# Linear attention with the routing of its tokens: the same steps in six slots instead of thirteen

## Chip, cores and metric

One core of one Trainium2 chip runs the whole kernel. The metric is the time of one execution on the device in microseconds; three runs before the change took 4580.45, 4585.04 and 4587.49, so the median is 4585.04.

## What is computed

The reference is a chain of sixteen residual blocks on 4096 tokens of 128 features (16 sequences of 256). Two neighbours matter here, a linear attention and the mixture of experts behind it:

```python
# linear attention (x is already normalised)
q = elu(x @ Wq.T) + 1;  k = elu(x @ Wk.T) + 1;  v = x @ Wv.T      # 16 heads of 8
kv = einsum('bhnd,bhne->bhde', k, v);  k_state = k.sum(axis=2)
attn = einsum('bhnd,bhde->bhne', q, kv) / max(q . k_state, 1e-6)
local = conv of width 3 over the sequence
return (attn + local) @ Wp.T + bp

# mixture of experts (x is already normalised)
logits = einsum('nc,ec->ne', xt, gate_w)                          # 8 experts
top_vals, top_idx = top_k(logits, 2);  top_w = softmax(top_vals)
expert e: (silu(xt @ w1[e].T) * (xt @ w2[e].T)) @ w3[e].T
out = sum over the two chosen experts of weight * expert(xt)
```

## The kernel before, in words

Activations stay on the chip, features on the partitions, in eight chunks of 512 tokens (two sequences each). `self.x` holds the residual stream, `self.ha` the normalised copy. A stage of the kernel is a list of steps, each a function of a chunk. `slots` (L1819) writes the order out by hand: in slot k, step i works on chunk k - i. The scheduler is told to keep this order (`manual_schedule`), and each engine then takes its instructions in the order in which they were written.

The linear attention (`linear`, L1947) has eight steps: three of the layer norm (`norm`: mean by a matmul, square, matmul, logarithm and exponential, multiply; for chunks 0 to 4 the stage before has done them, and they are empty), `project` (three projections, elu, the convolution), `sums` (k and v to `kv`), `heads` (q and `kv`, and the division), `join` (a transpose back, added to the convolution) and `out` (output projection, added to `x`).

Behind them come, as `last`, the eight steps that route the tokens to the experts. They are made by `Sending.steps` (L3545), and called "lead" steps, since they belong to the next block but are written into this stage:

- `norm(0)` to `norm(2)`, called `centre`, `spread` and `scale` below: the norm of the new `x`. Here the square is made on ScalarE.
- `compare` (L3566): the logits (TensorE), copied out on VectorE; `ahead`, which expert's logit is above which (VectorE, L3574), multiplied by a triangle on GpSimd (L3578); the maximum subtracted and `Exp` on ScalarE.
- `choose` (L3585): ranks from two sums over `ahead`, marks of the first and second expert, the two weights; all on VectorE down to the reciprocal (L3605), then two small instructions on GpSimd (L3606, L3607) that fill the weight and the token number into the row `out`.
- `place` (L3613): small matmuls count how many tokens went to each expert before this one; from that VectorE makes the row number `idx` (L3633).
- `turn` (L3636): four transposes of the normalised tokens, copied by ScalarE into `out`.
- `scatter` (L3645): eight indirect DMAs from GpSimd's queue (L3649), which write the 2 x 512 rows into the DRAM buffer `rows`, sorted by expert.

After the stage `table` (L3655) makes a small table, from which expert and row each tile of the experts starts, and `experts` (L2126) loads rows (L2145) and expert weights (L2147) through the queue of SyncE. Its first load waits for all rows to be stored.

So before, a chunk that enters at `project` in slot k is in `scatter` in slot k + 12: thirteen slots. Slot 2 is the first that has work (`project` of chunk 0), slot 22 the last (`scatter` of chunk 7). Within a slot, `slots` first writes the eight attention steps, the last one first, and then the eight lead steps, the last one first: `scatter`(c), `turn`(c+1), `place`(c+2), `choose`(c+3), `compare`(c+4), and so on. The number in brackets is the chunk.

Tiles rotate through small sets of buffers: two of most, three of `idx`, four of `out`; eight banks of the matmuls' result memory ("ps") are shared by all steps. A step that takes a buffer waits until its earlier reader is done.

Of the kernel before, what the change touches and what calls it, by code (L numbers as in the profile page):

```python
# [21 lines left out]
NCH = NT // CH  # L22
# [1627 lines left out]
class Fast(Net):  # L1650
# [168 lines left out]
    def slots(self, n, *steps, last=()):  # L1819
# [3 lines left out]
        with self.tc.manual_schedule():  # L1823
            self.logs()
            for k in range(n + len(both) - 1):
                for i in (*reversed(range(len(steps))), *reversed(range(len(steps), len(both)))):
                    if 0 <= k - i < n and k < n + len(both) - 1:
                        both[i](k - i)

    def lead(self, pool, bank="ps", tables=False):
# [114 lines left out]
    def linear(self, w):  # L1947
        x, h0 = self.x, self.ha
        nc = self.nc
        with ExitStack() as st:  # L1950
            p = self.stage(st, "n2", 2)
            qs, ks, kvs, os, ls = {}, {}, {}, {}, {}
            norm = [lambda c, i=i: self.norm_x_step(p, c, i) for i in range(3)]

            def elu1(ps, tag, bufs):
                e = p.tile([P, CH], F32, tag=tag, name=tag, bufs=bufs)
                self.act(e, ps, AF.Relu, scale=-1.0)
                self.act(e, e, AF.Exp, scale=-1.0)
                self.stt(e, ps, 0.0, e, ALU.max, ALU.add)
                return e  # L1960

            def project(c):
                s = self.chunk(c)
                pq, pk, pv = self.bank(), self.bank(), self.bank()
                self.mm(pq, w["Wq"], h0[:, s])
                for t in range(4):
                    ht = h0[:, c * CH + t * P : c * CH + t * P + P]
                    self.mm(pk[:, t * P : t * P + P], ht, w["Wk"])
                    self.mm(pv[:, t * P : t * P + P], ht, w["Wv"])
                qs[c] = elu1(pq, "q", 3)  # L1970
                k = elu1(pk, "k", 2)
                v = p.tile([P, 4, P + 1], F32, tag="v", name="v")
                self.act(v[:, :, :P], pv.rearrange("p (t d) -> p t d", t=4), AF.Copy)
                nc.gpsimd.memset(v[:, :, P:], 1.0)
                ks[c] = k, v
                l = p.tile([P, CH], F32, tag="l", name="l", bufs=4)
                lb, hb = self.bt(l), self.bt(h0[:, s])
                self.act(l, h0[:, s], AF.Identity, scale=w["conv_w"][:, 1:2], bias=w["conv_b"])
                self.stt(lb[:, :, 1:], hb[:, :, : T - 1], w["conv_w"][:, 0:1], lb[:, :, 1:], ALU.mult, ALU.add)
                self.stt(lb[:, :, : T - 1], hb[:, :, 1:], w["conv_w"][:, 2:3], lb[:, :, : T - 1], ALU.mult, ALU.add)  # L1980
                ls[c] = l

            def sums(c):
                k, v = ks.pop(c)
                pkv = self.bank()
                for b in range(2):
                    for u in range(2):
                        t = 2 * b + u
                        self.mm(pkv[:, b * 129 : b * 129 + 129], k[:, t * P : t * P + P], v[:, t], start=u == 0, stop=u == 1)

                kv = p.tile([P, 2, P + 16], F32, tag="kv", name="kv")
                src = pkv[:, :258].rearrange("p (b d) -> p b d", b=2)
                self.tt(kv[:, :, :P], src[:, :, :P], self.twice(self.k["blk8"]), ALU.mult)
                self.tt(kv[:, :, P:], src[:, :, P:].broadcast_to([P, 2, 16]), self.twice(self.k["blk8"][:, ::8]), ALU.mult)
                kvs[c] = kv

            def heads(c):
                q, kv = qs.pop(c), kvs.pop(c)
                o = p.tile([P, 4, P], F32, tag="o", name="o")
                for b in range(2):  # L2000
                    pn = self.bank()
                    for u in range(2):
                        t = 2 * b + u
                        self.mm(pn[:, u * 144 : u * 144 + 144], q[:, t * P : t * P + P], kv[:, b])
                    src = pn[:, :288].rearrange("p (u d) -> p u d", u=2)
                    rd = p.tile([P, 2, 16], F32, tag="rd", name="rd")
                    self.ts(rd, src[:, :, P:], 1e-6, ALU.max)
                    nc.vector.reciprocal(rd, rd)
                    self.tt(
                        o[:, 2 * b : 2 * b + 2].rearrange("p u (h d) -> p u h d", h=16),  # L2010
                        src[:, :, :P].rearrange("p u (h d) -> p u h d", h=16),
                        rd[:, :, :, None].broadcast_to([P, 2, 16, 8]), ALU.mult,
                    )
                os[c] = o

            def join(c):
                o, l = os.pop(c), ls[c]
                pt = self.bank()
                for t in range(4):
                    self.tr(pt[:, t * P : t * P + P], o[:, t])  # L2020
                self.tt(l, l, pt, ALU.add)

            def out(c):
                s = self.chunk(c)
                po = self.bank()
                self.mm(po, w["Wp"], ls.pop(c))
                self.stt(x[:, s], po, w["bp"], x[:, s], ALU.add, ALU.add)

            self.slots(NCH, *norm, project, sums, heads, join, out, last=self.lead(p))

    def mix(self, w):

# [1715 lines left out]
```

## Time and profile before

| | us |
|---|---|
| timed runs, median of three | 4585.04 |
| the profiled execution, its own time | 4544.11 |
| its span, first to last instruction | 4542.2 |
| TensorE busy in the span | 4023.2 (89%) |
| VectorE / ScalarE / GpSimd busy | 2543.9 / 2363.9 / 2140.4 |
| first matmul of `project`, chunk 0 | at 1937.70 |
| first store of `scatter` | at 2018.32 |
| end of the last store of this routing | at 2105.66 |
| first load of the experts | at 2107.20 |

All times "at" are counted from the start of the span. Timeline lines have the start, the busy time, the engine (PE is TensorE, DVE is VectorE, ACT is ScalarE, POOL is GpSimd, SPq the queue of SyncE), the line of the code, the operation, what it writes and reads, its shape, and in brackets how long the engine had been idle and for whom. A line can be that of a helper: L504 is every matmul, L508 every transpose, L528 every activation, L531 and L543 VectorE's two-input operations, L534 those of GpSimd. The other blocks of the kernel lie before 1937 and after 2107 and are not touched; a second routing, in the decay attention (2240 to 2600), uses the same lead steps in an order of its own and isn't touched either.

### The profile page before, as it was taken

To read this page: it belongs to the slowest core of one execution; us is meant where nothing else is said; L and a number is where in the kernel's file an instruction comes from. 1 tells how busy PE (TensorE), PEld (TensorE's weight loads), DVE (VectorE), ACT (ScalarE), POOL (GpSimd) and SP (SyncE) were. 2 spreads that over 40 slices of the span, in tenths; PEclk is the share of its full clock that TensorE was granted. 3 is DMA by queue.
4 is the path that set the end of the run, shared out by engine and by line. 5 is a ranking of instruction groups with operands and counts; after the bars stand their busy time and mean duration, and the time that the engine had idled before them with its cause. 6 is when DMAs were issued, how large, how long until landed. Compare 5 with 4: busy or idle time off the path is not lost. (4 is left out here: it accounts for less than half of the span.)

```text
span 4542.2 us, 70875 instructions
## 1 busy us (share of the span) xinstructions
PE 4023.2 (89%) x27720; PEld 2164.7 (48%) x27720; DVE 2543.9 (56%) x4437; ACT 2363.9 (52%) x4489; POOL 2140.4 (47%) x1848
## 2 busy tenths in 40 slices
PE   7999999999899899984989798969999888898868
PEld 3455455475455355453855486523333333444333
DVE  4764665363566476372356534637767565476354
ACT  6665466445766366552357533455555443764432
POOL 3653454231555265225424444658877576321241
PEclk9999999998999999986999899989999898999979
DMA  1800000000000000004510162000000000000000
GB/s 56 322 1 1 10 1 2 18 1 1 19 1 1 3 2 1 1 17 127 173 38 21 58 195 83 11 23 1 1 1 1 3 0 9 6 1 17 6 0 20
DMA packets 73078, 142.31 MB, mean 31 GB/s; under 512 B 11006, under 2 KB 42372, under 8 KB 72608
## 3 DMA queue, kind: packets, MB, share of 16 engines
q1 hardware_dynamic: 57120, 114.46, 7.5%
q0 software_dynamic: 9088, 16.94, 1.1%
q10 hardware_dynamic: 6528, 6.29, 0.5%
q8 instruction: 222, 3.64, 0.3%
q14 instruction: 120, 0.98, 0.1%
HBM read 84.22 MB, written 55.25 MB: 31 GB/s over the span
## 5 line engine op out<-in xcount | busy, mean ns | idle before, releaser
L528 ACT ACTIVATE pt<-ps 128x512 f32<-128x512 f32 (+1 forms) x896 | 422.2, 538 | 450.3 <-PE ps L504 446.2
L504 PE MATMUL ps<-hb,w 128*128 128x512 f32 (+1 forms) x960 | 483.1, 631 | 9.3 <-DVE hb L543 5.1
L504 PE MATMUL ps<-w,hb 128*128 128x512 f32 (+2 forms) x896 | 417.9, 580 | 18.7 <-DVE t L531 10.0
L531 DVE TENSOR_TENSOR t<-ps,tab 128x512 f32<-128x512 f32 x512 | 319.2, 684 | 196.3 <-ACT sq L528 193.5
L534 POOL TENSOR_TENSOR t<-t,ss 128x1024 f32<-128x1024 f32 x128 | 243.6, 1903 | 311.3 <-ACT ss L528 202.8
L534 POOL TENSOR_TENSOR t<-t,t 128x512 f32<-128x512 f32 x256 | 320.4, 1274 | 13.1 <-PE ps L504 10.1
L504 PEld LDWEIGHTS ps<-hb,w 128*128 128x128 f32 (+1 forms) x960 | 180.9, 197 | 286.5 <-issue 224.2
L534 POOL TENSOR_TENSOR nsq<-ha 128x512 f32<-128x512 f32 x128 | 145.3, 1136 | 336.9 <-ACT ha L528 315.7
L504 PE MATMUL ps<-nsq,ct 128*128 128x512 f32 x368 | 217.5, 676 | 74.2 <-POOL nsq L534 56.8
L531 DVE TENSOR_TENSOR u<-u,ps 128x512 f32<-128x512 f32 x220 | 129.3, 591 | 229.0 <-PE ps L504 172.2
L528 ACT ACTIVATE pt<-pt 128x768 f32<-128x768 f32 (+1 forms) x160 | 170.1, 1063 | 155.5 <-DVE pt L531 155.5
L2183 POOL DMA_INDIRECT back<-y,x x156 | 152.6, 978 | 198.0 <-ACT y L528 169.2
L504 PE MATMUL ps<-ot,w 128*128 128x512 f32 x448 | 211.8, 608 | 27.0 <-ACT ot L528 20.8
L504 PE MATMUL ps<-u,w 128*128 128x512 f32 (+1 forms) x448 | 221.9, 619 | 5.9 <-POOL u L534 5.9
L504 PE MATMUL ps<-qkt 64*128 64x192 f32 (+1 forms) x2048 | 216.4, 327 | 11.8 <-ACT pt L528 11.8
L504 PE MATMUL ps<-xt,w 128*128 128x256 f32 x936 | 219.5, 385 | 4.5 <-DMA w<-in_moe_x 3.5
L504 PEld LDWEIGHTS ps<-w,hb 128*128 128x128 f32 x896 | 149.4, 195 | 144.9 <-issue 102.4
L504 PEld LDWEIGHTS ps<-qkt 64*128 64x128 f32 x2048 | 153.6, 189 | 134.6 <-ACT qkt L528 51.5
L528 ACT ACTIVATE nrs<-ps,ct 128x512 f32<-128x512 f32 x208 | 140.7, 688 | 143.5 <-PE ps L504 140.7
L531 DVE TENSOR_TENSOR pt<-ps,w 128x384 f32<-128x384 f32 (+1 forms) x320 | 171.2, 576 | 73.6 <-PE ps L504 70.3
L531 DVE TENSOR_TENSOR ot<-ps,rd 128x512 f32<-128x512 f32 (+1 forms) x208 | 135.6, 652 | 135.9 <-ACT rd L528 106.6
L528 ACT ACTIVATE u<-ps,w 128x512 f32<-128x512 f32 x160 | 107.0, 685 | 185.1 <-PE ps L504 182.5
(360 smaller groups left out, 9012.9 us busy)
## 6 DMA issues: line engine op xcount, KB each, us to landing
w<-in_moe_x SPq DMA_DIRECT2D x78, 533.0 KB, 4.2
rows<-t SPq DMA_DIRECT2D x64, 520.0 KB, 11.1
x<-rows SPq DMA_DIRECT2D x78, 130.0 KB, 2.4
w<-in_local_f SPq DMA_DIRECT2D x8, 659.5 KB, 5.4
y<-back ACTq DMA_DIRECT2D x16, 256.0 KB, 3.2
y<-back SPq DMA_DIRECT2D x16, 256.0 KB, 3.2
w<-in_local_f SPq DMA_DIRECT2D x4, 658.5 KB, 7.2
back<-y,x POOLq DMA_INDIRECT x156, 2.8
```

The costliest lines, as they stand in the source:

```text
L504: self.nc.tensor.matmul(out, lhsT, rhs, start=start, stop=stop)
L528: self.nc.scalar.activation(out, in_, func, **kw)
L531: self.nc.vector.tensor_tensor(out, a, b, op)
L534: self.nc.gpsimd.tensor_tensor(out, a, b, op)
L2183: nc.gpsimd.indirect_dma_start(views[2 * i + t], bass.IndirectOffsetOnAxis(ap=x[:, t, C : C + 1].bitcast(I32), axis=0), y[:, t], None, bou ...
```

## The change

A new function writes the order of this stage. Its argument is one list of steps per slot of a chunk's way; in slot k set i works on chunk k - i. Within a slot it first writes the first step of every set (last set first), then the second step of every set, then the third.

```diff
+    def sets(self, n, *sets):
+        with self.tc.manual_schedule():
+            self.logs()
+            for k in range(n + len(sets) - 1):
+                for j in range(max(len(s) for s in sets)):
+                    for i in reversed(range(len(sets))):
+                        if j < len(sets[i]) and 0 <= k - i < n:
+                            sets[i][j](k - i)
...
-            self.slots(NCH, *norm, project, sums, heads, join, out, last=self.lead(p))
+            lead = self.lead(p)
+            sets = [norm[0]], [norm[1]], [norm[2], project], [sums, heads], [join, out, *lead[:1]]
+            self.sets(NCH, *sets, lead[1:4], lead[4:6], lead[6:])
```

With the names from above the eight sets are: norm 0; norm 1; norm 2 and `project`; `sums` and `heads`; `join`, `out` and `centre`; `spread`, `scale` and `compare`; `choose` and `place`; `turn` and `scatter`. A chunk that enters at `project` in slot k is now in `scatter` in slot k + 5, and the stage has 15 slots in place of 23. In slot k the order of writing is: `turn`(k-7), `choose`(k-6), `spread`(k-5), `join`(k-4), `sums`(k-3), norm 2, norm 1, norm 0; then `scatter`(k-7), `place`(k-6), `scale`(k-5), `out`(k-4), `heads`(k-3), `project`(k-2); then `compare`(k-5), `centre`(k-4). The steps themselves, their tiles and their buffers are as before.

## The prediction, made before the result was known

> **What bounds this part of the kernel now.** I read four views, in this order.
>
> First the busy time by stretch, cut by hand at the stage's own events: the first matmul of chunk 0's `project` (1937.70), the first indirect store (2018.32), the end of the last one (2105.66). Columns: length, busy time of each engine, granted TensorE clock, DMA share, GB/s.
>
> ```profile
> 1937.70:2018.30 80.60, 71.66 (x421) 52.28 (x420) 69.53 (x180) 48.46 (x86) 10.14 (x22) 0.96 0.03 10
> 2018.30:2105.70 87.40, 19.98 (x106) 14.41 (x106) 23.69 (x119) 14.46 (x29) 67.97 (x78) 0.53 0.15 49
> 2105.70:2190.00 84.30, 78.49 (x470) 67.86 (x471) 25.91 (x54) 31.18 (x74) 32.65 (x34) 0.95 0.67 210
> ```
>
> The stage has two halves. In the first VectorE and TensorE are nearly full and GpSimd is idle (10.1 of 80.6 us); in the second GpSimd alone works (68.0 busy of 87.4) and the others wait. Laying GpSimd's half under the first half is the whole prize.
>
> Second, GpSimd's own timeline inside one slot of the second half:
>
> ```profile
> 2040.20 0.21 POOL L534 TENSOR_TENSOR out<-out,e 128x4 f32<-128x4 f32 x1
> 2040.48 0.24 POOL L3607 TENSOR_SCALAR out<-ct 128x8 int32<-128x8 f32 x1
> 2040.80 0.72 POOL L534 TENSOR_TENSOR ahead<-ahead,ct 128x256 f32<-128x256 f32 x1
> 2041.68 1.06 POOL L3649 DMA_INDIRECT rows<-out,idx  x1 [0.15 <-issue]
> 2043.04 0.96 POOL L3649 DMA_INDIRECT rows<-out,idx  x1 [0.30 <-issue]
> ...
> 2050.99 0.95 POOL L3649 DMA_INDIRECT rows<-out,idx  x1 [0.30 <-issue]
> 2051.97 0.21 POOL L534 TENSOR_TENSOR out<-out,e 128x4 f32<-128x4 f32 x1
> ```
>
> A chunk's eight stores take 1.26 us each; from the first (2041.68) to the first instruction behind them (2051.97) is 10.3. With the three small instructions a slot is 2051.97 - 2040.20 = 11.8, gapless. The order matters: stores of chunk c, the two small ones of `choose`, then `compare`'s multiply.
>
> Third, VectorE in that slot:
>
> ```profile
> 2041.91 0.41 DVE L3589 TENSOR_REDUCE rank<-ahead 128x32 f32<-128x256 f32 x1
> ...
> 2044.43 0.18 DVE L3605 RECIPROCAL out<-g 128x4 f32<-128x4 f32 x1
> 2044.53 0.16 DVE L3571 COPY lg<-ps 128x32 f32<-128x32 f32 x1
> 2044.72 0.43 DVE L531 TENSOR_TENSOR ahead<-lg 128x256 f32<-128x256 f32 x1
> ```
>
> `choose` is 2044.61 - 2041.91 = 2.7 us on VectorE, and runs while GpSimd is busy with stores, so GpSimd never waits for it.
>
> Fourth, who waits for the last store:
>
> ```profile
> 2104.70 0.96 POOL L3649 DMA_INDIRECT rows<-out,idx  x1 [0.30 <-issue]
> 2107.20 0.41 SPq L2145 DMA_DIRECT2D x<-rows  x1
> ...
> 2109.63 0.66 PE L508 MATMUL ps<-ct,x 128*128 128x128 f32 x2 [32.45 <-DMA x<-rows]
> ```
>
> The experts' first load leaves 1.5 us after the last store and TensorE had waited 32 us for it. So the end of the last store, 2105.66, moves everything behind it one for one. The page's chain of waits was no use: its long pieces begin at 4249.
>
> **The change, part by part.** No instruction is added or removed; only the order changes, and each engine works its queue in program order. The eight copies of each step take the durations that the present rows show.
>
> *Gain: the first store comes sooner.* I follow chunk 0 through slots 2 to 7, at full clock, from the same start.
> - Slot 2 is as now: chunk 0's `l` is done on VectorE at 1943.5.
> - Slot 3: `heads`(0) now stands before `project`(1) on TensorE. `kv` 0.53 gives 1944.0, eight matmuls 1.15 give 1945.2. From `project`'s first matmul to the end of its last VectorE instruction the trace has 1942.66 to 1949.3, 6.6: 1951.8.
> - Slot 4: `join` 0.67, then `out`'s matmul 1.02 and `heads`(1) 1.0 (issue spacing) put `project`(2) at 1954.4, done 1961.0. `centre`'s copy and square on ScalarE stand behind `project` there: 1960.5.
> - Slot 5: `spread` 1.05, `join` 0.43, `sums` 0.97, the norm of chunk 5 0.86, `out` 0.86, `heads` 1.0 in TensorE's queue: `project`(3) starts 1965.6, done 1972.4; `compare` 0.6 on VectorE, 0.74 on GpSimd: 1973.7.
> - Slot 6: VectorE does `choose` to 1976.5. `Exp`, copy and square end 1974.5, then spread, join, sums, two norm matmuls 0.86 each, `place` 0.4, out, heads: `project`(4) at 1980.7, done 1987.5, `compare` done 1988.9.
> - Slot 7: Exp, copy, square to 1989.7; spread, join, sums, two norms to 1993.9; the copy of chunk 7's norm to 1995.2; its square on GpSimd, 1.1, to 1996.4. Only then comes store 1, since that square precedes it in GpSimd's queue.
>
> At full clock the first store is thus at 1996.4, 21.9 sooner. But in slots 5, 6 and 7 TensorE idles 4 us before each `spread` (`centre`'s matmul is over long before ScalarE's square). The trace shows what holes do here: after 2002.55 to 2005.08 without a matmul the clock fell to 0.50 until 2012, and the pair of `spread` took 2.08 instead of 1.13. On the path I have 5.0 + 6.2 + 4.2 us of TensorE before `project` and 2 x 2.5 in it, 20.4. Bounds: 0 (full clock) to +20.4 (half clock throughout). I take half, +10, because of the 11 us from 2005 to 2016 about 7 were at half clock (two-microsecond stretches of the first view): **first store at 2006.4, 11.9 sooner.**
>
> On the clock the Trainium skill ("TensorE: Matmul & The Clock Gate", Part 1) says that half clock follows about 3.4 us of idleness and ends after about 3.4 us of work. By that rule each slot would lose 1.7, in sum +5 instead of +10, and the total below +3. The trace's own stretch, at half clock for 7 us after a 2.5 us hole, is worse than the rule, so I stay with the row.
>
> *Loss: GpSimd now waits in every slot.* The new order in a slot is, for GpSimd: `choose`(c+1), stores of c, `compare`(c+2). `choose`(c+1) on VectorE needs `compare`(c+1)'s multiply, which is queued behind the eight stores of c-1; and the stores of c are queued behind the two GpSimd instructions of `choose`(c+1), which need VectorE's 2.7 us. Today `choose` is two slots ahead and hidden; here nothing hides it. Per slot: multiply 0.72, wake-up 0.08, choose 2.70, wake-up 0.08, two small ones 0.28 + 0.24, gap 0.28, together 4.4, plus 10.1 of stores = 14.5 against 11.6 to 11.8 now. Six slots (8 to 13) have it; slot 14 has the stores of chunk 7 alone. First store to last: 10.1 + 6 x 14.5 + 10.1 = 107.2, and three memsets of `project` of 0.1 behind stores: 107.5, **against 87.3 now: 20.2 longer.**
>
> Queued behind that wait is all of VectorE's slot: `join`, `kv`, `place`, `scale`, `out`, `heads`, `project`, `compare`, and TensorE behind `place`. From the start of `choose`, GpSimd reaches the next `compare` after 2.7 + 0.9 + 10.1 + 0.1 = 13.8. VectorE has it ready after `choose` 2.7, `join` 0.67, `out` 0.86 and `heads` 1.0 on TensorE, `project` 6.8 and 0.6: 12.7. So at full clock 1.1 us is to spare (3.4 in slot 7, which has no such wait ahead). Half clock makes TensorE's 4.4 us in it 8.8, 3.3 too late. With the clock mixed I count nothing; bounds 0 to +3 in slots 8 and 9 together.
>
> *Contention.* Stores now run beside a busy VectorE. All 128 stores of both routings lie at 0.954 / 0.958 / 1.437 us (minimum, median, maximum), and eight beside a busy VectorE in the decay stage (2518 to 2527) are 0.95 to 1.06. The few long ones here cost 0.18 to 0.48 more. Bounds 0 to 8 x 0.4 = 3; I take 0. What speaks against the change is the Trainium skill ("SBUF — State Buffer", SBUF: two separate sides): a VectorE instruction of some kinds locks GpSimd out, and a GpSimd-issued DMA that takes about 620 ns alone took about 3100. One such blockade per chunk would be 8 x 2.5, some +20; the stores in this trace show nothing of that size.
>
> *At no cost:* the routing table (ready 2.9 us of VectorE after `place`(7), near 2095, with chunk 7's stores still to come: hidden by 10 us of GpSimd); the weight loads that start when this stage frees their room (2013 for decay, not used before the experts are over); `idx`'s wait for landed stores, which held VectorE up to 7.1 us in a slot, goes, but it was hidden behind GpSimd.
>
> Sum: -11.9 + 20.2 = +8.3; I use **+8**. The profiled execution is 4544.1 (span 4542.2), so 4552 in a like profile; the timed runs' median 4585.04 is 0.9% above it, and the same 8 us on it give 4593. That is +0.17%: inside the 0.2% (9.2 us) that a measurement of this kernel can tell from no change, but near its edge.
>
> **The rivals.**
> 1. *The prize is won* (faster). GpSimd's slots stay at 11.7 because something lets `choose` run ahead of the stores: first store 1996.4 to 2006.4, plus 87.3: end at 2084 to 2094, -22 to -12, 4563 to 4573. For it: the second half's idle engines. Against: the queue order written in the diff, and no trace row where GpSimd passes over an instruction. 0.10.
> 2. *Half clock throughout* (slower). Slots 5 to 7 cost the other 10.4, and in the three slots that still have `project` VectorE, fed late by TensorE, sets the time rather than GpSimd: 3.3 each in slots 8 and 9, 4.4 - 3.4 = 1.0 in slot 7. +8 + 10.4 + 7.6 = +26; this decides once `choose` to `compare` takes over 13.8 us. Its range is +14 to +26, 4599 to 4611. For it: clock 0.53 in the present second half. 0.20.
> 3. *Full clock with the wait*: 1996.4 + 107.5 = 2103.9, -2, 4583. 0.10.
> 4. *The diff doesn't touch what ends the stage*, say the experts' load waits for something else by then: within 1 us of 4585. 0.05.
>
> **How the numbers follow.** My forecast, the wait with a mixed clock, has 0.55 and its own range +2 to +14, 4587 to 4599; about 0.33 of that is under +9.2. Slower by over 0.2%: 0.22 + 0.20 = 0.42. Within: 0.33 + 0.10 + 0.05 = 0.48. Faster: 0.10. The range for 8 in 10 holds the forecast, full clock, no effect and the nearer half of half clock: 4579 (with the 4 us by which before's runs reach under their median) to 4607. Left out: rival 1 and the far half of rival 2, 0.20.
>
> **What would show it.** The first store near 68.7 us after chunk 0's `project`, and six gaps of about 4.4 us on GpSimd between groups of eight stores, each ended by VectorE's reciprocal of `choose`: the wait is right. Groups 1.7 us apart: rival 1. GpSimd waiting longer than 4.4 us, for VectorE's `ahead`, and clock 0.5 before the first store: rival 2. I am wrong altogether if the first expert load does not follow the last store by about 1.5 us.

## The result, and the profile after

The changed kernel takes 4601.78 us (median of six, 4598.33 to 4605.04) against 4586.26 of the kernel before in the same comparison (six, 4580.45 to 4590.22): ratio 1.0036, interval 1.0025 to 1.0047, some 15 us slower. The forecast was +8, its range 4579 to 4607. Two later comparisons of the same two kernels, neither edited, gave 1.0014 (1.0005 to 1.0023) and 1.0024 (1.0013 to 1.0034).

One caution for reading the profiles: the same kernel before took about 4542 us in some comparisons and about 4588 in others, and I call their runs the 4542 runs and the 4588 runs. The profile of before shown above fits the first (4544.11), the profile after (execution 4598.36, span 4596.4) is of the second. So most of the 54 us between the two spans is not the change; the last section shows where they seem to lie. I therefore compare the stage itself: from chunk 0's sixteen small matmuls of `project` (1937.70 before) to the end of the last store of this routing.

| us | before | after |
|---|---|---|
| first store, from the stage's start | 80.6 | 66.2 |
| first store to end of the last | 87.3 | 113.4 |
| stage | 168.0 | 179.6 |
| GpSimd from the end of a group of eight stores to the next group, slot by slot | 1.5, 1.5, 1.5, 1.5, 0.8, 0.3, 0.3 | 4.4, 4.8, 10.5, 4.4, 4.4, 4.4, 0.3 |

The stage by halves in the profile after (length, busy time of PE, PEld, DVE, ACT, POOL, granted clock, DMA share, GB/s), cut at the first store as before:

```profile
1933.70:1999.90 66.20, 48.56 (x254) 34.82 (x253) 42.01 (x109) 30.70 (x53) 7.88 (x16) 0.87 0.01 1
1999.90:2113.30 113.40, 54.76 (x275) 37.99 (x273) 53.41 (x190) 33.52 (x61) 70.53 (x85) 0.66 0.14 44
```

VectorE's work did move under the stores (53.4 us of it behind the first store, 23.7 before). GpSimd has 70.5 us of work there (68.0 before), but now takes 113.4 for it. Its timeline says where the rest is (start, busy, engine, line, operation, shape, idle time and its releaser):

```profile
2023.69 0.96 POOL L3662 DMA_INDIRECT rows<-out,idx  x1 [0.30 <-issue]
2024.65 0.12 POOL L1985 MEMSET v<- 128x4 f32 x1
2025.08 0.72 POOL L534 TENSOR_TENSOR ahead<-ahead,ct 128x256 f32<-128x256 f32 x1 [0.31 <-issue]
2028.63 0.20 POOL L534 TENSOR_TENSOR out<-out,e 128x4 f32<-128x4 f32 x1 [2.83 <-DVE out L3618]
2028.90 0.24 POOL L3620 TENSOR_SCALAR out<-ct 128x8 int32<-128x8 f32 x1
2029.43 1.06 POOL L3662 DMA_INDIRECT rows<-out,idx  x1 [0.28 <-POOL out L3620]
...
2038.39 0.96 POOL L3662 DMA_INDIRECT rows<-out,idx  x1 [0.30 <-issue]
2039.34 0.13 POOL L1985 MEMSET v<- 128x4 f32 x1
2045.56 0.72 POOL L534 TENSOR_TENSOR ahead<-ahead,ct 128x256 f32<-128x256 f32 x1 [6.09 <-DVE ahead L531]
```

Read it downward. The stores of one chunk end at 2024.65. Only then can the multiply for the next chunk's `choose` run, then GpSimd idles 2.83 us until VectorE's reciprocal (L3618), does two small instructions, and the next stores leave at 2029.43. This is the predicted lock, 4.4 to 4.8 us, in five of the six slots. The last line is the sixth: 6.09 us more, for VectorE's `ahead`, which came late.

Most of why it came late stands on ScalarE (same columns):

```profile
2035.28 0.60 ACT L528 ACTIVATE q<-ps 128x512 f32<-128x512 f32 x1 [4.67 <-PE ps L504]
2035.90 0.63 ACT L528 ACTIVATE q<-q 128x512 f32<-128x512 f32 x1
2040.90 0.60 ACT L528 ACTIVATE k<-ps 128x512 f32<-128x512 f32 x1 [4.36 <-remote]
```

In `project` of chunk 7 ScalarE stands for 4.36 us ahead of k's activation. The profile gives "remote", that is, it finds nothing on this core that was waited for. TensorE had done the group of matmuls that k reads by 2037.81:

```profile
2035.74 2.07 PE L504 MATMUL ps<-w,ha 128*128 128x128 f32 x18
```

The experts still follow the last store (end 2113.28) after 1.5 us:

```profile
2114.74 0.41 SPq L2158 DMA_DIRECT2D x<-rows  x1
```

### The profile page after: what moved, and what is told of

Its sections match the earlier page's. It is cut to its first block, busy times and chain, and to the rows that moved or that the text cites. A ratio compares the mean times of both kernels' runs of the same rounds, so it can differ in the third digit from the quotient of the medians.

```text
span 4596.4 us, 70870 instructions
## 1 busy us (share of the span) xinstructions
PE 4048.5 (88%) x27720; PEld 2175.9 (47%) x27720; DVE 2542.4 (55%) x4437; ACT 2366.0 (51%) x4489; POOL 2142.6 (47%) x1848
```

## The experiments

Two theories. **The wait**: GpSimd's queue holds stores of c-1, the multiply for c+1, the two small ones of `choose`(c+1), stores of c; that order costs 4.4 us per slot and is why the stage got no shorter. **The clock** (the rival): TensorE's pauses in the six-slot order halve its clock, and late matmuls hold everything. All ratios are against the kernel before in the same set. The edits are to the changed kernel unless another is named. "Stage" and "first store" are as in the table above, from one profile each.

| kernel | first store | gaps between store groups | stage | ratio and interval |
|---|---|---|---|---|
| *set 1, kernel before 4542.81* | | | | |
| before_again | 80.6 | 1.5 1.5 1.5 1.5 0.8 0.3 0.3 | 168.0 | 1.0002 (0.9993 to 1.0011) |
| stores_first | 56.7 | 7.3 6.3 5.3 2.0 1.5 1.5 0.8 | 162.0 | 0.9987 (0.9978 to 0.9995) |
| ahead_on_vector | 66.1 | 0.9 5.8 6.0 1.6 0.8 0.8 0.3 | 162.9 | 0.9982 (0.9973 to 0.9991) |
| warm_clock | 63.2 | 4.4 4.9 4.4 4.4 4.4 4.4 0.3 | 170.8 | 1.0003 (0.9995 to 1.0012) |
| *set 2, kernel before 4541.93* | | | | |
| after_again | 68.9 | 4.4 4.4 4.9 4.4 4.4 4.4 0.3 | 176.6 | 1.0014 (1.0005 to 1.0023) |
| old_slots | 80.7 | 1.5 1.5 1.5 1.5 0.8 0.3 0.3 | 168.1 | 0.9999 (0.9990 to 1.0008) |
| five_slots | 48.6 | 3.2 3.2 3.6 1.5 1.5 1.5 0.8 | 145.1 | 0.9947 (0.9933 to 0.9960) |
| ahead_and_order | 52.9 | 2.5 2.3 2.4 0.8 0.9 0.8 0.8 | 144.4 | 0.9948 (0.9934 to 0.9961) |
| *set 3, kernel before 4587.78* | | | | |
| longer_choose | 66.6 | 5.7 7.8 9.3 5.7 5.7 5.7 0.3 | 186.4 | 1.0032 (1.0019 to 1.0045) |
| longer_choose_before | 83.6 | 1.5 1.5 1.5 1.5 0.8 0.3 0.3 | 171.0 | 1.0011 (1.0001 to 1.0020) |
| ahead_order_warm | 53.9 | 6.7 3.6 2.5 0.9 4.3 0.8 0.9 | 155.0 | 0.9989 (0.9980 to 0.9997) |
| after_third | 66.3 | 4.4 4.4 10.5 4.4 4.4 4.4 0.3 | 179.7 | 1.0024 (1.0013 to 1.0034) |

In the 4542 runs (sets 1 and 2) the stage explains the time almost one for one: ahead_and_order has a stage 23.6 shorter than before, and its ratio is worth -23.6 us (-30 to -18); stores_first -6.0 and -5.9; after_again +8.6 and +6.4 (+2.3 to +10.4).

**before_again: the kernel before, unedited.**

> The kernel before, unchanged, against itself: ratio 1.000 by every theory. Its profile is a second sample of the stage: if the 46 us by which the decay stage differs between the two profiles (2384 to 2587 before, 2394 to 2642 after) belong to the single execution and not to the change, the long decay stage, with ScalarE standing still several times ahead of raw, appears here too, and the span is near 4585 rather than 4542. If it belongs to the change, the decay stage is 203 us again. The stage of the change, from project's small matmuls of chunk 0 to the end of the last store, should be 168 us.

Stage and gaps of this kernel repeat to 0.1 us. The changed kernel repeats less well: with nothing edited its first store lies at 66.2, 68.9 and 66.3 in three profiles. So a difference of under 3 us ahead of the first store says little from one profile each; the plain gaps of 4.4 repeat to 0.1 us.

**stores_first: `turn` moved from the last set to the one before, so that `scatter` is alone in its set.** It is then the first step that a slot writes: GpSimd has the stores of c ahead of the two small ones of `choose`(c+1), not behind them.

```diff
-            self.sets(NCH, *sets, lead[1:4], lead[4:6], lead[6:])
+            self.sets(NCH, *sets, lead[1:4], lead[4:7], lead[7:])
```

> turn moves into the set of choose and place, scatter stands alone; still six slots. GpSimd's order in a slot becomes: stores of c, the two small instructions of choose(c+1), multiply of compare(c+2). Theory of the wait (GpSimd's order costs 2.8 us per slot because choose stands between two groups of stores): the six gaps of 4.4 us close to 1.5, the first store comes some 8 us sooner too because it no longer follows choose and the norm's square in its slot, the stage takes 162 to 169 us in place of 180, and the kernel is 11 to 17 us faster than the changed one, at or a little under the kernel before (4580 to 4590). Theory of the clock (TensorE at half clock is what makes the slots long): gaps of the same length appear elsewhere, VectorE still feeds each slot late, stage 175 to 180, kernel near 4600.

In its timeline the last store of a chunk and the first store of the next have only queued work between them:

```profile
2051.41 0.96 POOL L3662 DMA_INDIRECT rows<-out,idx  x1 [0.30 <-issue]
2052.39 0.21 POOL L534 TENSOR_TENSOR out<-out,e 128x4 f32<-128x4 f32 x1
2052.67 0.24 POOL L3620 TENSOR_SCALAR out<-ct 128x8 int32<-128x8 f32 x1
2053.46 0.72 POOL L534 TENSOR_TENSOR ahead<-ahead,ct 128x256 f32<-128x256 f32 x1 [0.55 <-DVE ahead L531]
2054.34 1.06 POOL L3662 DMA_INDIRECT rows<-out,idx  x1 [0.16 <-POOL ahead L534]
```

The wait for `choose` is gone, and the stage is 14.6 us shorter than after_again's. A miss: in the three slots that still hold a `project` the gap is 5.3 to 7.3 and not 1.5. There GpSimd now waits for VectorE, mostly for `ahead`: 4.95, 4.71 and 3.71 us. So without the lock the first three slots are bound by when VectorE is through with its own slot; how much of that is TensorE's lateness behind it is not split here.

**ahead_on_vector: the multiply by the triangle made on VectorE** (`self.quick` is true around this stage only), the order unchanged. GpSimd's queue then has nothing that `choose` needs.

```diff
-            net.gt(ahead.rearrange(flat), ..., ALU.mult)
+            (net.tt if net.quick else net.gt)(ahead.rearrange(flat), ..., ALU.mult)
```

> In this stage alone the multiply of ahead by the triangle is done by VectorE (0.42 us) and not by GpSimd (0.72); the order is that of the changed kernel. Theory of the wait: choose no longer depends on anything queued behind the stores, so its 2.7 us run beside the stores before; GpSimd's gap between groups falls from 4.4 to about 1, the stage to 164 to 171 us, the kernel 8 to 15 us under the changed one. Theory of the clock: TensorE and VectorE are as late as before, 0.35 us more of VectorE per slot; stage 178 to 182, kernel at 4600.

Where a plain gap had GpSimd waiting 2.83 us for the reciprocal, it now waits 0.78:

```profile
2058.89 0.20 POOL L534 TENSOR_TENSOR out<-out,e 128x4 f32<-128x4 f32 x1 [0.78 <-DVE out L3620]
```

Gaps without `project` in the slot fall from 4.4 to between 0.8 and 1.6, the stage to 162.9: breaking the lock at its other link closes the same waits. Two gaps of 5.8 and 6.0 stay, which the expectation did not have, again with `project` in the slot, and again ended by VectorE (GpSimd waits 4.88 and 5.09 us for it).

**warm_clock: four extra matmuls in every slot of `centre`, into a bank that nobody reads**, to fill TensorE's pause ahead of `spread`.

```diff
+            def warm(c):
+                pw = self.bank()
+                for _ in range(4):
+                    self.mm(pw, w["Wq"], x[:, self.chunk(c)])
+
-            sets = ..., [join, out, *lead[:1]]
+            sets = ..., [join, out, *lead[:1], warm]
```

> Adds, after centre in each slot, four matmuls of 512 columns that nobody reads (3.5 us of TensorE at full clock, in its pause), so that the clock is kept up; the output is not touched. Theory of the clock: granted clock near 1.0 up to the last project, first store 5 to 9 us sooner than 66 us after project's small matmuls, no late ahead in the slot of the last project, stage 168 to 174. Theory of the wait alone: the six gaps of 4.4 us stay, clock or not; the stage stays at 175 to 181. Both act together if the first store comes sooner and the gaps stay: that is what I expect, stage 170 to 176, kernel 4 to 10 us under the changed one.

The halves of its stage (columns as above):

```profile
1937.00:2000.20 63.20, 54.84 (x276) 36.75 (x277) 42.02 (x109) 30.71 (x53) 7.85 (x15) 0.95 0.01 1
2000.20:2107.80 107.60, 65.17 (x315) 41.10 (x313) 52.80 (x190) 33.52 (x61) 70.56 (x85) 0.78 0.15 47
```

The clock up to the first store rises to 0.95, from 0.85 in after_again and 0.87 in the first profile after, and the first store comes 5.6 us sooner than in the one and 3.0 than in the other; the 3.0 is hardly more than the changed kernel's own spread. But from there to the end it is 107.5 against after_again's 107.7: the gaps of 4.4 do not care about the clock. So the clock has a part in where the chain starts, and the wait sets its length.

**after_again, after_third: the changed kernel, unedited, once among the 4542 runs and once among the 4588 runs.**

> The changed kernel, unchanged, on the chip of the other runs of this call, beside the kernel before. What is open: in its first profile ScalarE stood still for 4.4 us in the stage (releaser given as remote) and six times, 53 us, in the decay stage, and the gap ahead of the store group of chunk 3 was 10.6 us instead of 4.4. If those stops come with the chip or the execution, they are gone here: the third gap is 5 to 7 us (4.4 of the wait and what half clock makes VectorE late), the stage 174 to 177 us, the kernel 6 to 9 us over the kernel before (ratio 1.0013 to 1.0020), and the decay stage takes 203 us. If they come with the change, third gap 10.6, stage 180, decay stage 249 us and a ratio of 1.003 or more.

> The changed kernel a third time, for the spread between chips and executions: 1.0014 again, a third gap near 5 and a stage of 176 to 178 if nothing stops ScalarE; if this chip has the stops of the first profile, a span 40 us or more longer for this kernel and the kernel before alike, and a ratio between 1.001 and 1.004.

after_again has no ScalarE stop in the stage. Its third gap is 4.9, not 10.5. after_third has the stop at the same instruction as the first profile, k's activation of chunk 7:

```profile
2049.28 0.60 ACT L528 ACTIVATE k<-ps 128x512 f32<-128x512 f32 x1 [4.33 <-remote]
```

**old_slots: the new function, one step per slot**, the order of before's thirteen slots in the new code.

```diff
-            sets = ...
-            self.sets(NCH, *sets, lead[1:4], lead[4:6], lead[6:])
+            self.sets(NCH, *[[f] for f in (*norm, project, sums, heads, join, out, *lead)])
```

> The new function with one step in each set: sixteen sets, the thirteen slots of before, and only the order inside a slot is the new one (the eight routing steps now ahead of the attention's, instead of behind). GpSimd's order is that of before: stores of c, choose(c+3), compare(c+4). Theory of the wait: no gap over 1.6 us, first store 80 to 84 us after project's small matmuls, stage 166 to 171, same as before within 0.1%. If the order of the routing against the attention steps (and not the few slots) were what cost time: 174 or more.

Stage 168.1 and ratio 0.9999: the new function costs nothing by itself. What matters is which steps share a slot and in what order.

**five_slots and ahead_and_order: `scatter` alone in its set, as in stores_first, and the other steps shared out differently**, so that the slot with `project` holds less. The first has only other lists; the second also makes the multiply on VectorE.

```diff
# five_slots
+            sets = [norm[0]], [norm[1]], [norm[2], project, sums], [heads], [join, out, *lead[:2]]
+            self.sets(NCH, *sets, lead[2:4], lead[4:7], lead[7:])
# ahead_and_order
+            self.sets(NCH, *sets, lead[1:3], lead[3:7], lead[7:])
```

> Grouping of the steps chosen so that no group of stores has a choose ahead of it and VectorE's work of a slot is shorter: sums joins project, heads stands alone, spread joins join, out and centre; scale and compare; choose, place and turn; scatter alone. Theory of the wait: gaps of 1.5, first store near 52 us after project's small matmuls, stage 148 to 156, kernel 0.25 to 0.45% under the kernel before. Theory of the clock alone: stage 165 to 175, no gain on stores_first.

> Both remedies: the multiply of ahead on VectorE, and compare, choose, place and turn in one set with scatter alone in the last (spread and scale in the set ahead); six slots. GpSimd then has only stores, the two small instructions and the memsets. Theory of the wait: store groups follow at 0.8 us or VectorE's slot, whichever is longer; first store near 55 us, stage 144 to 150, kernel 0.4 to 0.5% under the kernel before. If the two remedies remove the same wait and nothing else: no better than the better of them alone, 162.

Both beat both kernels: 0.9947 (0.9933 to 0.9960) and 0.9948 (0.9934 to 0.9961), a little more than expected. A miss in five_slots: its first three gaps are 3.2 to 3.6 and not 1.5, and its stage is under the expected 148 only since the first store comes at 48.6 and not near 52. Two consecutive boundaries in ahead_and_order, one of a slot with `project` and one without:

```profile
2023.46 0.32 POOL L3622 TENSOR_SCALAR out<-ct 128x8 int32<-128x8 f32 x1
2023.83 0.10 POOL L1985 MEMSET v<- 128x4 f32 x1
2025.15 1.07 POOL L3664 DMA_INDIRECT rows<-out,idx  x1 [1.21 <-DVE ahead L531]
...
2034.10 0.98 POOL L3664 DMA_INDIRECT rows<-out,idx  x1 [0.30 <-ACT out L528]
2035.11 0.21 POOL L534 TENSOR_TENSOR out<-out,e 128x4 f32<-128x4 f32 x1
2035.40 0.24 POOL L3622 TENSOR_SCALAR out<-ct 128x8 int32<-128x8 f32 x1
2035.92 1.06 POOL L3664 DMA_INDIRECT rows<-out,idx  x1 [0.28 <-POOL out L3622]
```

GpSimd waits 1.21 us in the one and 0.28 in the other, and the stores run nearly back to back, from 52.9 us after the stage's start. The prize that the two halves of the stage promised, up to -22 in rival 1, was there.

**longer_choose, longer_choose_before: VectorE's second sum in `choose` (0.6 us) made three times over**, with the same result, in the changed kernel and in the kernel before.

```diff
-            nc.vector.tensor_reduce(won, ...)
+            for _ in range(3 if net.quick else 1):
+                nc.vector.tensor_reduce(won, ...)
```

> The changed kernel with a longer choose in this stage: one of its two sums over ahead (0.60 us on VectorE) is made three times instead of once, with the same result, so choose takes 1.2 us more. Theory of the wait: every microsecond of choose stands in GpSimd's gap; the six gaps grow from 4.4 to 5.6, the first store comes 2.4 later (two chooses ahead of it), the stage takes 176.6 + 9.6 = 186. If VectorE's whole slot or the clock set the gaps: gaps of 4.4 in the slots without project, stage 177 to 180.

> The same 1.2 us in the kernel before, where choose lies beside the stores. Theory of the wait: the gaps between store groups stay at 1.5 and below; only the three chooses ahead of the first store cost, in a first half where VectorE is nearly full: first store and end 3.6 us later, stage 171 to 172. If choose were not hidden before: stage 176 or more.

This is the sharpest test, since it prices the wait. A plain gap in the changed kernel with the longer `choose`:

```profile
2070.94 0.74 POOL L534 TENSOR_TENSOR ahead<-ahead,ct 128x256 f32<-128x256 f32 x1
2075.78 0.20 POOL L534 TENSOR_TENSOR out<-out,e 128x4 f32<-128x4 f32 x1 [4.11 <-DVE out L3621]
```

GpSimd waits 4.11 in place of 2.83, and plain gaps grow from 4.37 to 5.65: each of the 1.28 us added to `choose` appears in the gap. In the order of before the gaps stay at 1.5, and the stage is 3.0 longer than in the kernel before in the 4542 runs, nearly all of it ahead of the first store. So there the longer `choose` stays beside the stores.

The stage of the changed kernel, 186.4, is the number that was expected, but not by the expected parts. The first store was to come 2.4 later and did not: 66.6, against 66.3 in after_third. In two early slots the gap grows by more than 1.28, to 7.8 and 9.3, since VectorE's longer slot also makes the next `ahead` late (GpSimd waits 2.04 and 3.55 us for it). That the two misses cancel is luck. Against after_third, which has a stop in the stage, the stage grows by 6.8. The whole kernel's 1.0032 can't be told from after_third's 1.0024, so what prices the wait is the plain gaps.

**ahead_order_warm: ahead_and_order and the four matmuls of warm_clock.**

```diff
-            sets = ..., [join, out, *lead[:1]]
+            sets = ..., [join, out, *lead[:1], warm]
```

> The fastest so far (multiply of ahead on VectorE, scatter alone) with the four matmuls per slot that nobody reads. Theory of the clock: its three gaps of 2.3 to 2.5 us ahead of the store groups of chunks 1 to 3 come from slots that TensorE makes late at half clock; they close to 0.9 and the first store comes some 3 us sooner: stage 136 to 142. If TensorE has no long pause left there, the added 3.5 us per slot cost instead: stage 145 to 155.

A miss for the theory of the clock: 155.0 against 144.4 without the four matmuls. In it, one of the 4588 runs, ScalarE is standing still twice inside the stage, for 7.4 us in sum, and VectorE once for 3.7:

```profile
2032.80 0.60 ACT L528 ACTIVATE ha<-ps 128x512 f32<-128x512 f32 x1 [1.20 <-remote]
...
2081.57 1.09 ACT L528 ACTIVATE out<-ps 128x512 f32<-128x512 f32 x2 [6.20 <-remote]
```

But the gaps that grew are the first, second and fifth, by 9.0 us in sum, and none of these stops lies in them. What the trace shows ahead of them is the added work itself. In this grouping `warm` is written ahead of `compare`, so its matmuls stand in TensorE's queue directly before the logits; ahead of the fifth gap, for one:

```profile
2043.34 3.60 PE L504 MATMUL ps<-x,w 128*128 128x512 f32 x8
2046.77 0.95 PE L504 MATMUL ps<-w,ha 128*128 128x8 f32 x8
```

The logits start 3.9 us after the transposes of `turn` here, and 0.4 us after them in a like slot of ahead_and_order. That is the other case that the expectation named, 145 to 155. The two kernels ran in different sets, so the price is not exact. The run gives no support for a further gain from the clock.

## Why the prediction came out as it did

The measured 4601.78 lies in the stated range, but above the 4587 to 4599 that the prediction gave its own forecast: it lies in the range of rival 2, and the stated range holds it since it took in the nearer half of that rival. Point by point, with after_again (of the 4542 runs, which the prediction's profile fits) and the first profile after (of the 4588 runs).

- **What ends the stage** (the last store, then 1.5 us to the experts' first load): right. 1.5 us again, and stage and time move together in sets 1 and 2. Rival 4 is out.
- **The wait on GpSimd, 4.4 us in six slots**: right. 4.36 to 4.43 in the plain ones, with the releaser as foretold; longer_choose shows its size comes from `choose`, stores_first and ahead_on_vector that the queue order makes it. Rival 1 falls for this kernel; the time that it promised came in the two that avoid that order.
- **The first store at 68.7 us**: 68.9 in after_again, 66.2 and 66.3 in the other two. The number was right, its parts less so. At clock 0.95 (warm_clock) it came at 63.2, not near the 58.7 that I had walked out for full clock. So the clock cost about 3.0 to 5.6 rather than 10, and some 4.5 of other time was missing from the walk; the four added matmuls may account for part of that, and I have not split it. That the two errors cancel is luck. What was measured is nearer the +5 that the prediction had estimated from the Trainium skill's rule ("TensorE: Matmul & The Clock Gate", Part 1) and set aside; the total by that estimate is about +3.3, not below +3. Rival 2 asked for +20.4 here and a clock of 0.5, and fails; rival 3 asked for full clock, and warm_clock, the nearest to it, has a stage of +2.8 and not -2.
- **Contention beside a busy VectorE, 0 of 0 to 3**: right. Three of the 64 stores after are above 1.1 us (1.19, 1.33, 1.43); three of before are (1.13, 1.34, 1.44). A blockade of some 2.5 us a chunk, which the prediction estimated from the figures of the Trainium skill's "SBUF — State Buffer", does not appear: the longest store of this routing in any of the fourteen profiles is 1.44 us.
- **Late VectorE in slots 8 and 9, 0 of 0 to +3**: this is the term that was mis-sized, where the result was taken. There the third gap is 10.5, that is 6.1 over the plain 4.4 and twice what the upper bound allowed. In after_again the same gap is 4.9, so 0.5 late, inside the bounds. Counted from the first store of the group ahead of it, the two traces split the 5.6 between the gaps. From q's first activation to k's it is 5.6 us in place of 1.6: 4.1 for ScalarE's stop. From the store to q's activation it is 5.9 in place of 4.6: 1.2 for TensorE, whose granted clock stayed at 0.52 (2029.2 to 2032.9) where the like stretch of after_again has 0.89. The remaining 0.3 is a longer store in after_again. The matmuls of `sums` show the clock, first in the profile after, then in after_again:

```profile
2029.86 1.93 PE L504 MATMUL ps<-v,k 128*128 128x129 f32 x8
```

```profile
2036.04 1.14 PE L504 MATMUL ps<-v,k 128*128 128x129 f32 x8
```

  The 1.2 is what rival 2 named, late matmuls that hold VectorE, 1.2 of the 3.3 that it asked for in this slot. The slack that the prediction had worked out for this chain, 1.1 us at full clock, covers neither. That is read from the traces of two runs with the stop (after_third has the same) and one without; no run takes the stop alone away.
- **The sum**: predicted -11.9 and +20.2, +8.3 for the stage. Measured -11.7 and +20.4 in after_again, +8.6 (ratio 1.0014, +6.4 us, interval +2.3 to +10.4). Where the result was taken it is -14.4 and +26.1, +11.6: the late third gap was in part hidden by a first store that came 2.5 sooner than foretold. The remaining 4 of the result's 15.5 lie inside what repeated comparisons of the same kernel gave there: the third set's 1.0024 (1.0013 to 1.0034) is some 11 us, and its interval overlaps the result's.

**The theory that stands**: the in-order queue of GpSimd ties two chunks together, and that adds 20.4 us from the first store to the last (107.7 against 87.3, after_again) where 11.7 were gained ahead of the first. The clock is a smaller part: 3.0 to 5.6 us ahead of the first store, and behind it 1.2 us in the third gap of the result's profile. **Open**: why ScalarE stops.

## What to carry to other kernels

When steps are put into fewer slots, write down for each engine's queue, in order, the long group of one chunk, then everything up to the long group of the next; if anything in between depends on work of another engine that itself depends on something queued behind the first group, that chain is paid in full in every slot. Moving one step to the other side of the long group, or one small instruction to another engine, takes that wait away: here one position in a list turned +0.14% (0.05 to 0.23) into -0.13% (-0.22 to -0.05), and dividing the slots more evenly into -0.5%. And where the slack left in a slot is 1 us, a stop of several us on an engine of that chain goes into the gap, as 4.1 us did here.

## What the runs showed of the hardware

In all five profiles of the 4588 runs (set 3 and the result) ScalarE stands still at places where the profile names nothing on the core, the longest 9.4 us; VectorE does it now and then (7.0 us, in after_third). None of the nine profiles of the 4542 runs, six with a reordered stage and three in the order of before, has one. The largest such waits of ScalarE in the decay stage (2380 to 2650), first in the profile after, then in longer_choose_before (us in total, times, longest):

```profile
ACT raw L528 <- remote: 53.0, 6, 9.4
```

```profile
ACT raw L528 <- remote: 47.6, 6, 9.3
```

In after_again the same view of the same stretch has no such row. The second kernel has the order of before, so these 48 to 53 us are not of the change. They are about the 46 us by which the 4588 runs and the 4542 runs differ for the kernel before; that they make up that difference is likely, not shown. The stops that I followed in the profile after lie beside a group of eight indirect stores and end within 1.6 us of the group's end: the store group of the stage ends at 2039.35 and ScalarE goes on at 2040.90; in the decay stage 2408.38 and 2408.57, 2446.43 and 2446.63. What it waits for is not shown by any run, and was not tried. Nor is it shown to be a matter of the chip: set 1 (4542.81) and set 3 (4587.78) are recorded under the same chip number, 12, and set 2 (4541.93) under 10. What follows for measuring: the same kernel before takes 4542 in one set and 4588 in another, so a kernel is to be compared with a kernel before of its own set.
